# Four results of each block-product unit stored from GpSimd's queue instead of SyncE's

## The chip, the cores and the metric

The kernel runs on one core of one Trainium2 chip. The metric is device time in microseconds (us) of one execution. Three runs of the kernel before gave 3406.56, 3407.65 and 3411.39 us, so the median is 3407.65 us. A smaller number is better.

## The reference, cut to what matters

The input is `x` of 16 batches by 256 tokens by 512 channels, in fp32. Layer 0 is a decoder block: self attention, cross attention and an MLP. Layer 1 is an RWKV block: token mixing, a linear recurrence over the tokens, a gate and a channel mixing. The part that the change touches is the recurrence, with 32 heads of 16 channels:

```
def step(s, inp):
    k_l, v_l, w_l, r_l = inp
    a = k_l[..., :, None] * v_l[..., None, :]
    out = jnp.einsum('bhs,bhst->bht', r_l, faaaa * a + s)
    s_new = a + w_l[..., None] * s
    return (s_new, out)
```

The kernel does not step through 256 tokens. It cuts them into blocks of 8. Inside of a block it forms all products of r, k and the decays w directly; from block to block it carries the state with a scan. For each block the first part leaves four results:

- `rp`: r times the product of the decays from the block's start to the token;
- `ks`: k times the product of the decays from the token to the block's end;
- `tot`: the product of all eight decays of the block;
- `y`: what the block's own tokens add to the output.

## The kernel before, in words

Everything is recorded first as operations with a cost, an engine or a choice of engines, and the tiles read and written. A planner (`Sched.run`, L260) then places them one after the other: at each step it takes the operation that can start first by its own cost table, picks the engine where there is a choice, gives the tile a buffer, and emits the instruction. Each engine and each DMA queue runs its instructions strictly in that order. The planned costs therefore decide the order of all queues, and a changed cost in one place moves instructions far from it.

The phases are A (self attention), B (cross attention), C (MLP), D (token mixing: r, k, v, w, g to scratch in HBM) and E (the tail: state scan, gate, output projection, channel mixing). C and D are cut in two halves of eight batches: C0, D0, C1, D1. Between them runs a side stream of 16 units, recorded by `intra` (L1167): one unit covers four batches (`g`) and 128 channels (`q`). A partition holds one block of 8 tokens, so a tile is 128 blocks by 8 tokens by 128 channels in fp32, 512 KB. Units 1 to 8 (phase `I0`) run beside C1, units 9 to 16 (phase `I1`) beside the tail.

One unit loads K, R and W (L1188), multiplies K by the bonus `u` and by R (L1207, L1208), and doubles the reach of the decays in three rounds (L1212 to L1243). The products are recorded with `tt`, which is `sub` at L489: the planner puts them on VectorE (DVE) or on GpSimd (POOL), and in the trace all carry the line of `sub`, L492 for POOL. The reductions (L1209, L1213, L1222, L1239, L1254) are on DVE alone. After the third round the unit loads V (L1240), stores `rp`, `ks` and `tot` (L1244), forms the eight rows of Y (L1246 to L1256; the last one ends with a reduction on DVE, L1254) and stores `y` (L1257). `rp`, `ks` and `y` are 512 KB in rows of 512 bytes, `tot` is 64 KB.

All DMAs go through `dma` (L479). It records an operation on SP with a planned cost of 440 ns and emits `nc.sync.dma_start`; its line in the trace is L480. SP's queue holds 1218 DMAs, the loads of weights, of the units and of the tail among them, and the 64 stores of the units. When the DMA at its head waits for the engine that makes its data, those behind it wait too. The tiles K, R, W, V of the units have the tag `rk` with a quota of four (L1624), so the planner lets a next unit's load follow once a tile of the unit before was given up.

The tail reads back what the units stored, four units at a time since it works by batch with all channels: `states` loads `ks` (L1400) and `tot` (L1364), `reads` loads `rp` (L1450), `heads` loads `y` (L1479). Batches 12 to 15 need units 13 to 16.

Of the kernel before, what the change touches and what calls it, by code (L numbers as in the profile page):

```python
# [16 lines left out]
B, S, C = 16, 256, 512  # L17
# [168 lines left out]
class Sched:  # L186
# [73 lines left out]
    def run(self):  # L260
# [13 lines left out]
        def can(o):  # L274
            n = {}
            for h in o.tiles:
                if h.cls is not None and h.t is None:
                    k = h.phase, h.tag, h.cls
                    n[k] = n.get(k, 0) + 1
            for h in o.tiles:  # L280
                if h.cls is not None and h.t is None:
                    k = mem.why_not(h, n[h.phase, h.tag, h.cls])
                    if k is not None:
                        return k
            return None

        def put(o):
            k = can(o)
            if k is not None:
                waits.setdefault(k, []).append(o)  # L290
                return
            banks, t0 = 0, o.hold
            for h in o.tiles:
                if h.cls is not None and h.t is None:
                    t0 = max(t0, mem.ready(h))
                    banks += h.cls == "p"
            if banks > 1:
                t0 = max(t0, sorted(mem.banks.values())[banks - 1])
            o.t0 = {}
            for e, _, _ in o.alts:  # L300
                o.t0[e] = t0
                for d in o.deps:
                    p = ops[d]
                    o.t0[e] = max(o.t0[e], p.end + (self.SAME[e] if p.eng == e and not p.xfer else p.lat + self.LATE.get(e, 0.0)))
            for a in o.alts:
                ready[a[0]].append((o, a))
# [5 lines left out]
        while done < len(ops):  # L312
            best = None
            for e in engs:
                f, c = free[e], None
                for o, a in ready[e]:
                    s = o.t0[e] if o.t0[e] > f else f
                    if e in o.port and port > s:
                        s = port
                    if o.xfer and queues - self.AHEAD > s:  # L320
                        s = queues - self.AHEAD
                    for h in o.banks:
                        for e2, t in used.get(h, {}).items():
                            if e2 != e and t > s:
                                s = t
                    if len(o.alts) > 1:
                        s += o.bias.get(e, 0.0)
                    kx = (max(s - o.urge, f), o.prio, a[1])
                    if c is None or kx < c[0]:
                        c = (kx, o, a)  # L330
                if c is not None and (best is None or c[0] < best[0]):
                    best = c
            assert best is not None, "the streams block each other: " + str({k: [o.i for o in v][:3] for k, v in waits.items() if v})
            _, o, alt = best
            for a in o.alts:
                ready[a[0]].remove((o, a))
            k = can(o)
            if k is not None:
                waits.setdefault(k, []).append(o)
                continue  # L340
            o.eng, o.cost, fn = alt
            o.lat = self.LAT[o.eng]
            t0 = max(o.hold, o.t0[o.eng])
            woken = {}
            for h in sorted((h for h in o.tiles if h.cls is not None and h.t is None), key=lambda h: h.seq):
                if h.cls is not None and h.t is None:
                    t0 = max(t0, mem.ready(h))
                    mem.put(h)
                    woken[h.phase, h.tag, h.cls] = 1
            s = max(t0, free[o.eng])  # L350
            for h in o.banks:
                s = max([s] + [t for e2, t in used.get(h, {}).items() if e2 != o.eng])
            if o.eng in o.port:
                s = max(s, port)
                port = s + o.cost
            if o.xfer:
                s = max(s, queues - self.AHEAD)
            o.start, o.end = s, s + o.cost
            free[o.eng] = o.end
            for h in o.banks:  # L360
                used.setdefault(h, {})[o.eng] = o.end + o.lat
            if o.xfer:
                o.end = queues = max(o.end + self.START, queues) + o.xfer
            if not self.dry:
                fn()
                self.pin()
            for h in o.tiles:
                h.left -= 1
                if h.left == 0 and h.cls is not None:
                    mem.drop(h, o.end + o.lat)  # L370
                    woken[h.phase, h.tag, h.cls] = 1
                    woken[mem.SIZE[h.cls][0]] = 1
            done += 1
            for d in o.outs:
                p = ops[d]
                p.ndep -= 1
                if p.ndep == 0:
                    put(p)
            for k in woken:
                for p in waits.pop(k, []):  # L380
                    put(p)
# [21 lines left out]
def c_dma(nbytes, short=False):  # L403

    return nbytes / (146.0 if short else 290.0)


class Kern:
# [67 lines left out]
    def cols(self, ap, n, name):  # L476
        return self.konst([128, n], ap.rearrange("(k p) -> p k", p=128), name)

    def dma(self, h, out, in_, nbytes, r=(), w=None, short=False):  # L479
        o = self.emit("SP", 440.0, lambda: self.nc.sync.dma_start(out=out(), in_=in_()), r=r, w=[h] if w is None else w)  # L480
        o.xfer = c_dma(nbytes, short)
        return o

# [683 lines left out]
def intra(self, g, q, hin, hout, after, early=None):  # L1167
# [6 lines left out]
    def view(ap, t=8):  # L1174
        return bass.AP(tensor=ap.tensor, offset=ap.offset + g * 4 * S * C + q * 128, ap=[[8 * C, 128], [C, t], [1, 128]])
# [6 lines left out]

    def store(n, t, f, nb):
        h, ap = hout[n]
        self.dma(None, lambda: view(ap) if n != "tot" else bass.AP(tensor=ap.tensor, offset=ap.offset + g * 128 * C + q * 128, ap=[[C, 128], [1, 128]]), f, nb, [t], [(h, (g, q))])

    A = tile("A", [128, 8, 8, 8], "A")
    K, R, W = load("k"), load("r"), load("w")  # L1188
# [30 lines left out]
    for h in range(2):  # L1219
        o = 4 * h  # L1220
# [14 lines left out]
    for h in range(2):  # L1235
        o = 2 * h
# [5 lines left out]
    tt(512, lambda: K[:, 0:4], lambda: K[:, 0:4], lambda: W[:, 4:5].to_broadcast([128, 4, 128]), [K, W], [K])  # L1242
    tt(128, lambda: W[:, 0], lambda: W[:, 0], lambda: W[:, 4], [W], [W])  # L1243
    store("rp", R, lambda: R(), 524288), store("ks", K, lambda: K(), 524288), store("tot", W, lambda: W[:, 0], 65536)  # L1244
    yield
    Y = tile("Y", [128, 8, 128], "Y")  # L1246
    for t in range(8):
        n = t + 1
# [6 lines left out]
        if t in (3, 5):  # L1255
            yield  # L1256
    store("y", Y, lambda: Y(), 524288)  # L1257


# [481 lines left out]
```

## Time and profile before

| what | value |
|---|---|
| median of three runs | 3407.65 us |
| time of the profiled execution | 3407.0 us |
| its span, first to last instruction | 3405.2 us |
| granted TensorE clock, mean | 0.975 |
| PE busy | 3196.5 us, 94% |
| DVE busy | 2842.5 us, 83% |
| ACT busy | 1878.1 us, 55% |
| POOL busy | 1501.6 us, 44% |
| stores of the units, all on SP | 16 each of `s_rp`, `s_ks`, `s_y`, `s_tot` |
| first and last `s_rp` store | 2088.0 and 3136.3 us |

The span is what the trace covers; the execution's own time is 1.8 us longer. An engine's busy share is an average over stages with different limits: POOL's 44% is made of stretches with almost nothing and of stretches at 94%. What a change costs or gains is therefore read from the stretch in which it lies, and from what the next engine waits for there. A row like `POOL slot L492 <- DMA slot<-s_w` names the waiting engine, what its instruction writes and its line, and behind the arrow what it waited for: here a load from the scratch tensor `s_w`. `SPq` is SP's DMA queue.

### The profile page before, as it was taken

The page shows a single profiled execution, that of the slowest core. Times are in us where ns is not written, and L with a number is a line of the kernel's source. Part 1 is how long each engine was busy: PE and PEld are TensorE (multiplying, and loading weights), DVE is VectorE, ACT ScalarE, POOL GpSimd, SP SyncE. Part 2 cuts the span into 40 slices and gives each one's busy share as a digit, 9 for nine tenths or more (in the row PEclk, how much of TensorE's full clock was granted, in tenths as well). Part 3 has the DMA queues.
Part 4 walks back from the last instruction along what each step waited for, and adds up shares of the span by engine and source line. Part 5 has one row for each costly group of instructions (what it writes and reads, how often), then busy time and mean ns, then how long its engine had stood idle before and what let it go on. Part 6 is the DMA issues. An engine that isn't in the chain of part 4 may idle for free. (4 is left out here: it accounts for less than half of the span.)

```text
span 3405.2 us, 73366 instructions
## 1 busy us (share of the span) xinstructions
PE 3196.5 (94%) x27210; PEld 2627.1 (77%) x27210; DVE 2842.5 (83%) x6701; ACT 1878.1 (55%) x4750; POOL 1501.6 (44%) x1932
## 2 busy tenths in 40 slices
PE   7999999999999999899999999999799859999899
PEld 5788777777777777799998888999698745555577
DVE  7888888888888888876788889899889868888786
ACT  6666666666666666633334554434454547565654
POOL 3444444443444444300021127898112766767442
PEclk9999999999999999899999999999899969999999
DMA  3000000121111111310023554434345876765530
GB/s 101 26 26 32 27 29 28 35 79 44 45 45 45 45 45 54 104 33 13 32 75 125 170 180 131 124 117 121 106 152 160 251 230 189 211 195 177 172 120 32
DMA packets 321775, 334.21 MB, mean 98 GB/s; under 512 B 40294, under 2 KB 225166, under 8 KB 321418
## 3 DMA queue, kind: packets, MB, share of 16 engines
q1 hardware_dynamic: 321418, 329.52, 31.1%
q8 instruction: 216, 3.54, 0.4%
q14 instruction: 141, 1.16, 0.1%
HBM read 198.32 MB, written 131.10 MB: 97 GB/s over the span
## 5 line engine op out<-in xcount | busy, mean ns | idle before, releaser
L743 POOL TENSOR_SCALAR slot<-slot,k_rin 128x256 f32<-128x256 f32 x1024 | 489.2, 496 | 619.1 <-DVE k_rin L740 582.7
L492 POOL TENSOR_TENSOR slot<-slot,slot 128x512 f32<-128x512 f32 (+10 forms) x428 | 570.6, 1352 | 339.5 <-ACT slot L571 96.3
L737 ACT ACTIVATE slot<-slot,k_nmx 128x256 f32<-128x256 f32 x1024 | 507.8, 500 | 171.0 <-DVE k_nmx L736 148.5
L506 PE MATMUL bank<-slot,block 128*128 128x256 f32 x2048 | 584.8, 286 | 1.8 <-ACT slot L487 1.3
L507 PE MATMUL bank<-slot,block 128*128 128x256 f32 x2048 | 581.9, 284 | 2.1 <-DVE slot L578 1.4
L508 PE MATMUL bank<-slot,block 128*128 128x256 f32 x2048 | 580.9, 284 | 0.0
L506 PE MATMUL bank<-block,slot 128*128 128x512 f32 x1240 | 502.4, 405 | 4.4 <-DVE slot L577 2.9
L487 ACT ACTIVATE slot<-bank 128x512 f32<-128x512 f32 (+2 forms) x634 | 343.1, 571 | 291.0 <-PE bank L508 148.8
L508 PE MATMUL bank<-block,slot 128*128 128x512 f32 x1240 | 486.6, 392 | 4.5 <-DVE slot L578 2.7
L507 PE MATMUL bank<-block,slot 128*128 128x512 f32 x1240 | 486.4, 392 | 0.0
L506 PEld LDWEIGHTS bank<-slot,block 128*128 128x128 f32 x2048 | 393.5, 192 | 10.6 <-ACT slot L487 3.0
L507 PEld LDWEIGHTS bank<-slot,block 128*128 128x128 f32 x2048 | 393.6, 192 | 9.8 <-DVE slot L623 1.8
L736 DVE CUSTOM_DVE_ANT_0 slot<-slot,slot 128x256 f32<-128x256 f32 x1006 | 398.6, 443 | 0.0
L508 PEld LDWEIGHTS bank<-slot,block 128*128 128x128 f32 x2048 | 393.5, 192 | 0.0
L730 DVE SCALAR_TENSOR_TENSOR slot<-bank,slot 128x512 f32<-128x512 f32 x512 | 330.0, 680 | 53.4 <-PE bank L768 25.1
L756 PE MATMUL bank<-k_c,slot 128*128 128x128 f32 x2048 | 286.3, 280 | 17.6 <-POOL slot L743 13.4
L756 PEld LDWEIGHTS bank<-k_c,slot 128*128 128x128 f32 x2048 | 229.8, 142 | 88.5 <-POOL slot L743 57.5
L506 PE MATMUL bank<-slot,slot 128*128 128x256 f32 (+1 forms) x848 | 276.8, 326 | 13.9 <-ACT slot L577 11.5
L506 PEld LDWEIGHTS bank<-block,slot 128*128 128x128 f32 x1240 | 234.6, 189 | 65.4 <-issue 19.8
L507 PE MATMUL bank<-slot,slot 128*128 128x256 f32 (+1 forms) x848 | 275.5, 325 | 6.6 <-DVE slot L578 6.3
L508 PEld LDWEIGHTS bank<-block,slot 128*128 128x128 f32 x1240 | 233.8, 189 | 59.1 <-DVE slot L578 5.1
L508 PE MATMUL bank<-slot,slot 128*128 128x256 f32 (+1 forms) x848 | 275.0, 324 | 2.4 <-DVE slot L578 2.4
(203 smaller groups left out, 6467.7 us busy)
## 6 DMA issues: line engine op xcount, KB each, us to landing
slot<-in SPq DMA_DIRECT2D x153, 256.0 KB
slot<-x SPq DMA_DIRECT2D x64, 512.0 KB
x<-slot SPq DMA_DIRECT2D x48, 512.0 KB
slot<-in SPq DMA_DIRECT2D x32, 512.0 KB
sdr<-slot SPq DMA_DIRECT2D x128, 128.0 KB
slot<-sdr SPq DMA_DIRECT2D x32, 512.0 KB
s_k<-slot SPq DMA_DIRECT2D x16, 512.0 KB
s_w<-slot SPq DMA_DIRECT2D x16, 512.0 KB
```

The lines of the kernel that those rows point to most:

```text
L487: self.emit(("ACT", "DVE"), (c_act(n), c_dve(n)), (lambda: nc.scalar.activation(out=out(), in_=in_(), func=AF.Copy), lambda: nc.vector.ten ...
L492: self.emit(("DVE", "POOL"), (c_dve(n), c_pool(n)), (lambda: nc.vector.tensor_tensor(out=out(), in0=in0(), in1=in1(), op=op), lambda: nc.g ...
L506: nc.tensor.matmul(o, lhsT=lh, rhs=rh, start=first and i == 0, stop=False)
L507: nc.tensor.matmul(o, lhsT=lh, rhs=rl, start=False, stop=False)
L508: nc.tensor.matmul(o, lhsT=ll, rhs=rh, start=False, stop=last and i == k - 1)
L730: emit("DVE", c_dve(512), lambda j=j, T=T: nc.vector.scalar_tensor_tensor(out=T(), in0=ps[j](), scalar=-scale, in1=mask(), op0=ALU.mult, o ...
L736: emit("DVE", c_dve(256) + 80, lambda T=T, j=j, qt=qt: nc.vector.tensor_tensor_reduce(out=T[:, qt, :], in0=T[:, qt, :], in1=negb[:, qt, :] ...
L737: emit("ACT", c_act(256, 1, 1), lambda T=T, Et=Et, j=j, qt=qt: nc.scalar.activation(out=Et[:, qt, :], in_=T[:, qt, :], func=AF.Exp, scale= ...
L743: emit("POOL", 470, lambda jj=jj, qt=qt: nc.gpsimd.tensor_scalar(out=E[jj][:, qt, :], in0=E[jj][:, qt, :], scalar1=rin[:, qt, jj : jj + 1] ...
L756: nc.tensor.transpose(pt[:, k, 128 * qt : 128 * qt + 128], E[j][:, qt, 128 * k : 128 * k + 128], self.ident())
```

## The change

`dma` gets a flag `own`. With it the DMA is recorded on POOL with a planned cost of 1100 ns, and emitted with `nc.gpsimd.dma_start`. The unit's `store` sets the flag for `y`, `rp`, `ks` and `tot`, which is for all four. The planner's allowance behind a transfer (`LAT`) is kept at SP's 950 ns for any DMA, where POOL's own table entry is 65 ns. No data, size or address changes.

```
-            o.lat = self.LAT[o.eng]
+            o.lat = self.LAT["SP" if o.xfer else o.eng]
...
-    def dma(self, h, out, in_, nbytes, r=(), w=None, short=False):
-        o = self.emit("SP", 440.0, lambda: self.nc.sync.dma_start(out=out(), in_=in_()), r=r, w=[h] if w is None else w)
+    def dma(self, h, out, in_, nbytes, r=(), w=None, short=False, own=False):
+
+        e, c, q = ("POOL", 1100.0, self.nc.gpsimd) if own else ("SP", 440.0, self.nc.sync)
+        o = self.emit(e, c, lambda: q.dma_start(out=out(), in_=in_()), r=r, w=[h] if w is None else w)
         o.xfer = c_dma(nbytes, short)
         return o
...
     def store(n, t, f, nb):
         h, ap = hout[n]
-        self.dma(None, lambda: view(ap) if n != "tot" else bass.AP(...), f, nb, [t], [(h, (g, q))])
+        own = n in ['y', 'rp', 'ks', 'tot']
+        self.dma(None, lambda: view(ap) if n != "tot" else bass.AP(...), f, nb, [t], [(h, (g, q))], own=own)
```

The changed file is three lines longer below these places. In the two built programs the instructions stand as follows. SP's queue goes from 1218 to 1154 DMAs. POOL goes from 1932 to 1984 instructions: 64 DMAs more and 12 compute instructions fewer. DVE goes from 6701 to 6716, ACT from 3725 to 3722, PE stays at 21546. The streams are the same up to the end of the first unit; from there on they are in another order on every engine, PE included (of 16090 rows of PE's stream, equal neighbours merged, the first that differs is 11202).

More of the change, by code (lines that the diff above doesn't have):

```diff
@@ L1184, in store @@
         h, ap = hout[n]
-        self.dma(None, lambda: view(ap) if n != "tot" else bass.AP(tensor=ap.tensor, offset=ap.offset + g * 128 * C + q * 128, ap=[[C, 128], [1, 128]]), f, nb, [t], [(h, (g, q))])
+        own = n in ['y', 'rp', 'ks', 'tot']
+        self.dma(None, lambda: view(ap) if n != "tot" else bass.AP(tensor=ap.tensor, offset=ap.offset + g * 128 * C + q * 128, ap=[[C, 128], [1, 128]]), f, nb, [t], [(h, (g, q))], own=own)
     A = tile("A", [128, 8, 8, 8], "A")
```

## The prediction

> **What bounds the kernel now.** I read first the profile's slices, then the engines by stretch, then SP's waits, then one unit on POOL and SP in order of time, and last the chain.
>
> ```profile
> PE   7999999999999999899999999999799859999899
> POOL 3444444443444444300021127898112766767442
> DMA  3000000121111111310023554434345876765530
> ```
>
> A slice is 85 us. The units lie in slices 25 to 28 (2088 to 2400 us, beside the MLP) and 32 to 37 (the tail). PE is full in the first stretch; the tail is where it has holes.
>
> ```profile
> core 0: us, PE busy (x) PEld busy (x) DVE busy (x) ACT busy (x) POOL busy (x), PEclk, DMA share, GB/s
> 2200.00:2300.00 100.00, 99.81 (x640) 90.73 (x639) 92.47 (x133) 39.41 (x72) 93.94 (x72) 1.00 0.41 123
> 2300.00:2400.00 100.00, 99.62 (x646) 90.81 (x645) 95.17 (x141) 44.18 (x81) 79.07 (x64) 1.00 0.36 109
> 2400.00:2500.00 100.00, 79.28 (x452) 68.85 (x451) 82.03 (x152) 48.59 (x92) 16.23 (x20) 0.88 0.41 130
> 2700.00:2800.00 100.00, 56.60 (x1204) 46.35 (x1202) 70.54 (x121) 50.90 (x119) 64.83 (x60) 0.69 0.78 234
> 3000.00:3100.00 100.00, 91.63 (x1372) 61.27 (x1371) 86.95 (x160) 70.67 (x155) 69.74 (x64) 0.95 0.62 191
> ```
>
> So the first eight units run on a POOL that has little room (79 to 94%), under a PE that never stops; the second eight run on a POOL that is some 70% busy, under a PE that is 57 to 92% busy. Next, what SP's queue waited for, in each stretch, and what that made late:
>
> ```profile
> SPq L480 <- POOL slot L492: 150.8, 27, 21.6
> SPq L480 <- DVE slot L1254: 60.9, 15, 8.7
> ...
> SPq L480 <- POOL slot L492: 57.7, 14, 10.7
> SPq L480 <- DVE slot L1254: 14.4, 3, 8.4
> ...
>   POOL slot L492: 27.6, 6
> ...
> PE bank L1419 <- DMA block<-s_v: 29.2, 6, 14.2
> ```
>
> The first two lines are 2088 to 2650 us, the next two the tail: stores at the head of SP's queue that wait for POOL's product or DVE's last reduction of Y. Behind them stand the next unit's loads; the fifth line, of those who waited for the tensor s_w, says that POOL waited 27.6 us in all for a load of W. The last line is PE in the tail, waiting for loads that the units have no part in. Then the last unit, in order of time along the chain:
>
> ```profile
> 3133.78 2.51 POOL slot L492 x2
> 3136.31 3.51 DMA s_rp<-slot
> 3139.87 3.67 DMA slot<-s_rp
> ...
> 3146.29 6.76 POOL slot L492 x5
> 3153.05 3.53 DMA s_ks<-slot
> 3156.59 5.20 DMA slot<-s_ks
> 3161.82 0.88 DVE slot L1346 x2
> 3163.09 1.11 PE bank L1371 x4
> ```
>
> POOL finishes a product, the store lands, the tail loads it back, and only then PE goes on. From 3120 to 3163 us PE was busy 32.81 of 43 us. The last unit is thus on the path: if it comes later, the end comes later by nearly as much.
>
> **The price of a store on POOL.** No row of before has a DMA on POOL. From below the nearest is the same transfer issued by SP: 0.56 us for a store of rp, ks or y (medians 563, 558 and 555 ns). From above it is POOL's own pass over as many elements as a store moves, the product with `u` over 128x1024 fp32: 2.41 us in the first stretch. A store issues 1024 rows of 512 bytes, but computes on no element. Between ends a factor of four apart I take the geometric middle, 1.2 us, for all four stores; the tot store is a sixteenth of the rows, but its SP issue had a median of 1.24 us. Four stores: 4.8 us per unit, bounds 2.2 and 9.6.
>
> The Trainium skill, "DMA: Bandwidth & Descriptors", section "Latency and other measured facts", puts the first byte at about 1 us for a DMA from GpSimd and about 0.6 us from SP. By it alone, the two landings of the last unit would be 0.8 us later together. Against the change speaks "SBUF — State Buffer", section "SBUF: two separate sides", in its box on the trap that DVE blocks DMA: a two-port VectorE instruction keeps GpSimd from writing descriptors, and a DMA of about 620 ns took about 3100 ns beside one. The trace has DVE at 92 to 95% in the first stretch, but no run here shows such a block. By that rule the 64 stores would cost 64 x 2.5 = 160 us more of POOL.
>
> **The waits that move to POOL.** POOL runs in order. On SP the y stores waited 75.3 us in 18 waits for L1254, 4.7 us per unit. In the changed order most y stores stand behind some products of the next unit, so most of it passes under work; I keep a third, 1.5 us per unit (bounds 0 and 4.7). Behind the waiting store stand the next unit's products and the tail's other POOL work (L1346, L596), for which ACT, DVE and at last PE wait.
>
> **What the loads gain.** Freed of stores, K, R, W and V can issue sooner. POOL waited 27.6 us for W, 10.6 us for K and 1.6 us for R: 39.8 us in 16 units, 2.5 per unit. Their place still follows the planner's quota of four tiles, so I take half, 1.2 us per unit (bounds 0 and 2.5).
>
> **First stretch.** Net 4.8 + 1.5 - 1.2 = 5.1 us per unit, eight units 41 us. The `s_rp` stores were issued from 2088.0 to 2366.55 us, a period of 39.8 us, of which POOL was idle 14% (42.4 us of 2100 to 2400), 5.6 us per unit. Part of that idle is the very wait for W, part is waiting for DVE; I let half of the 41 be swallowed. The eighth unit then ends 20 us later. PE does not need it there: the covering work is the MLP's matmuls (99.6% busy) and it ends at 2400. What it meets is the change of phase at 2400 to 2500, where PE already lost 20.7 us, and whose buffers and POOL work come after the units in the queues. A third of the slip reaches PE: 7 us (bounds 0 and the whole 41).
>
> **Tail.** Again 41 us for units 9 to 16. The `s_rp` issues from 2901.3 to 3136.3 us are 58.8 us apart, and POOL is some 70% busy, so 17 us per unit are idle. If all idle could be used the slip is 0; if each idle piece is a wait inside the unit's own chain it is 41. I take half, 20 us, and it goes to the end one for one, by the chain above.
>
> **The last unit's stores.** Its ks now stands before the products of Y on POOL, and rp and tot behind them. Before it was the other way round: rp at 3136.31, ks at 3153.05. So the last thing that the tail waits for stands at the same place, plus a tot store ahead of it (1.2 us) and 0.6 us more issue: 2 us.
>
> **SP's own relief.** SP loses 48 x 0.56 + 16 x 1.24 = 47 us of issue. It counts only where PE waits for an SP load, 2700 to 2800 us, with 0.78 of the DMA engines' time taken. Five stores were issued there, 3.3 us: -3 us. The data to move stays, so I expect no more.
>
> The rule of the Trainium skill, "DMA: Bandwidth & Descriptors", section "Issuing engines are not separate DMA queues", says that another issuing engine saves only the sequencer's time. By it alone the sum would be -3 us.
>
> **The new order.** From the first unit's end on every engine's stream is resorted: 12 products move off POOL, DVE gets 15 instructions more. The same matmuls remain. What a resorting can give or take lies in the PE holes of the tail, 98 us from 2700 to 3300; I set it at 0, plus or minus 15.
>
> Sum: 7 + 20 + 2 - 3 = 26 us on the profiled execution's 3407.0 us: 3433. That execution is 0.65 us under the median of the runs, so 3434 us.
>
> **The rivals.**
> *Faster: the loads come early.* One mechanism: SP, without waiting stores, runs ahead, and the units lose all 39.8 us of load waits while PE loses most of its 29.2 us. For it: 150.8 us of SP waits on POOL alone. Against: in 2700 to 2800 the DMA engines are the limit, and POOL gets 4.8 us per unit of new work. It decides when POOL's price per store is below 0.6 us. Then 8 x (2.4 - 2.5) is nothing for the tail, and PE gains half of 29.2, with resorting some 20: 3387 us.
> *No change: all is swallowed.* POOL's 17 us of idle per unit take the 5.1 us, and the phase change hides the rest: 3407 plus or minus 7.
> *Much slower: a store costs POOL 2.4 us or more.* Then 9.6 + 1.5 - 1.2 = 9.9 us per unit, 79 us per half. With POOL at 94% in the first stretch nothing more is swallowed there; tail 60, first stretch 25, last unit 5: 3497 us. More is possible if DVE holds POOL off.
> That the stores do not move is excluded by the built program: 64 DMAs stand in POOL's stream.
>
> **How the numbers follow.** Chances: forecast 0.67, much slower 0.17, no change 0.06, faster 0.10. The forecast alone spans 3415 to 3465: bounds of the swallowed half in the tail (0 and 41) and of the resorting. Leaving out a tenth at each end, the range is 3404 to 3490. Within 0.2% (6.8 us) is what a measurement of this kernel can hardly tell from no change. Slower 0.84, same 0.06, faster 0.10.
>
> **What would show it.** Right: 48 DMAs on POOL at about 1.2 us each; the first stretch's unit period near 42 to 43 us instead of 39.8; the last unit's stores at 3165 to 3180 instead of 3136 to 3155; the time from the last store to the end unchanged at some 250 us. SP's waits on POOL L492 and DVE L1254 gone, waits of POOL on DVE L1254 in their place. Wrong: a price under 0.6 us, POOL waits for W, K and R at zero and a last unit no later than 3155 (faster or same), or POOL above 95% from 2100 to 2400 with units 45 us or more apart (much slower).

## The result and the profile after

Four runs of the changed kernel gave 3440.88, 3450.06, 3451.16 and 3451.22 us, a median of 3450.61 us. Four runs of the kernel before (the three above and one of 3410.71 us) gave a median of 3409.18 us. The ratio is 1.0111, with a 95% interval of 1.0096 to 1.0126: the change costs some 38 us by the ratio, 41 us by the medians. The profiled execution took 3451.16 us, its span is 3449.4 us, the mean granted clock 0.970 (0.975 before).

The slices of the changed kernel, in tenths of busy time. A slice is 86 us.

```profile
PE   7999999999999999899999999999699769988889
...
POOL 3444444444444444200021128898213766768442
...
DMA  3001001021111111300024563333444876655530
```

The last twelve digits of PE are 699769988889, before 799859999899: seven of them are below 9 where four were. The tail is where to look. The engines by stretch, in the changed kernel:

```profile
core 0: us, PE busy (x) PEld busy (x) DVE busy (x) ACT busy (x) POOL busy (x), PEclk, DMA share, GB/s
2200.00:2300.00 100.00, 98.52 (x620) 88.11 (x620) 90.31 (x129) 33.09 (x59) 90.54 (x71) 1.00 0.38 112
2300.00:2400.00 100.00, 98.17 (x643) 89.33 (x642) 91.19 (x138) 41.88 (x76) 89.56 (x76) 1.00 0.37 113
2400.00:2500.00 100.00, 72.68 (x392) 61.56 (x391) 84.86 (x147) 45.85 (x86) 33.88 (x32) 0.85 0.41 127
2700.00:2800.00 100.00, 63.85 (x1178) 54.23 (x1181) 74.06 (x121) 59.56 (x135) 62.39 (x56) 0.72 0.81 249
3000.00:3100.00 100.00, 84.59 (x1245) 55.33 (x1246) 81.94 (x146) 58.73 (x140) 65.70 (x60) 0.91 0.63 188
...
3100.00:3200.00 100.00, 75.74 (x958) 47.24 (x957) 73.83 (x119) 48.40 (x103) 75.21 (x66) 0.89 0.54 165
```

The table of before has no row for the last stretch. It is this one:

```profile
3100.00:3200.00 100.00, 89.72 (x788) 53.51 (x787) 82.78 (x159) 55.81 (x127) 56.86 (x56) 0.93 0.59 182
```

Read the PE column against the table of before. Beside the MLP PE loses some 1.3 us per 100 from 2200 us on (98.52 for 99.81, 98.17 for 99.62); from 2100 to 2200 us, which the tables leave out, it loses 6.2 (93.80 for 99.99). At the change of phase it loses 6.6 us (72.68 for 79.28), from 3000 to 3100 us 7.0, and from 3100 to 3200 us 14.0, the most of all. From 2700 to 2800 us it gains 7.3. Over the whole span PE was busy 3208.7 us for the same 27210 instructions, before 3196.5. So 32 of the 44 us by which the span grew are idle time of PE; no run tells what made its busy time 12 us longer.

What SP's queue waited for, first from 2088 to 2650 us, then (the last two lines) in the tail from 2650 to 3300 us:

```profile
SPq L482 <- DVE slot L893: 107.7, 7, 22.4
SPq L482 <- DVE slot L1257: 83.8, 8, 28.3
...
SPq L482 <- POOL slot L494: 1.8, 8, 0.2
...
SPq L482 <- PE bank L1422: 77.5, 13, 14.7
...
SPq L482 <- POOL slot L494: 3.9, 7, 1.3
```

The waits on POOL's product (L494, which was L492) went from 150.8 and 57.7 us to 1.8 and 3.9. SP did not become free by that. In all it waited 484.4 us in the first stretch and 325.8 in the tail, before 467.5 and 307.5: its wait for L1257 (L1254 before) grew from 60.9 to 83.8 us although no `y` store is left in the queue, and in the tail its wait for L1422 (L1419 before) grew from 31.5 to 77.5 us. At the head stands now a load that waits for a buffer.

POOL's own waits: the stores of `y` from 2088 to 2650 us, and, from the view of the tensor `s_w`, what is left of the wait for W:

```profile
POOL s_y L482 <- DVE slot L1257: 12.1, 2, 11.4
...
  POOL slot L494: 1.7, 1
```

The wait for W went from 27.6 to 1.7 us. In its place POOL waited 17.6 us in 4 waits for DVE's last reduction of Y, over the whole run. PE in the tail:

```profile
PE bank L1461 <- DVE slot L1359: 12.9, 2, 11.2
PE bank L1422 <- ACT slot L1349: 10.1, 2, 9.8
PE bank L1422 <- ACT slot L1430: 9.7, 1, 9.7
...
PE bank L1422 <- DMA block<-s_v: 5.2, 3, 2.5
```

The wait for `s_v` went from 29.2 to 5.2 us, as an earlier load would do it. But three waits of about 10 us each, on results of DVE and ACT, stand in its place; before, the longest wait of PE on DVE or ACT in this stretch was 7.4 us.

The price of a store on POOL, from the views of the four scratch tensors (minimum, median, maximum in ns):

```profile
L482 POOL DMA_DIRECT2D s_rp<-slot x16: 841/881/982, 2106.6 to 3190.8; - x16
...
L482 POOL DMA_DIRECT2D s_ks<-slot x16: 816/888/922, 2105.4 to 3179.9; - x16
...
L482 POOL DMA_DIRECT2D s_y<-slot x16: 834/862/1030, 2104.4 to 3192.6; - x16
...
L482 POOL DMA_DIRECT2D s_tot<-slot x16: 579/597/762, 2107.4 to 3190.2; - x16
```

All 64 cost 16 x (0.881 + 0.888 + 0.862 + 0.597) = 52 us of POOL. The last stores went out at 3179.9 to 3192.6 us; before, they went out at 3136.3 to 3155.3. POOL's stream around them, in order of time:

```profile
3164.48 0.69 POOL L1349 TENSOR_SCALAR slot<-slot,k_em 128x512 f32<-128x512 f32 x1 [8.19 <-DMA slot<-sdr]
...
3171.48 7.62 POOL L494 TENSOR_TENSOR slot<-slot,slot 128x1024 f32<-128x1024 f32 x5
3179.20 0.72 POOL L598 TENSOR_TENSOR k_lnrs<-k_lnrs,k_mhalf 128x2 f32<-128x2 f32 x1
3179.88 0.90 POOL L482 DMA_DIRECT2D s_ks<-slot  x1
...
3182.97 7.30 POOL L494 TENSOR_TENSOR slot<-slot,slot 128x512 f32<-128x512 f32 x5
3190.21 0.59 POOL L482 DMA_DIRECT2D s_tot<-slot  x1
3190.80 0.90 POOL L482 DMA_DIRECT2D s_rp<-slot  x1
3192.59 0.84 POOL L482 DMA_DIRECT2D s_y<-slot  x1 [0.90 <-DVE slot L1257]
```

The stores themselves take 3.2 of these 29 us. Above the last unit's products stands an operation of the tail, L1349, that waited 8.19 us for a load of the tail.

A slip is best followed by one kind of event that every version has in the same number. The table gives how much later than in the kernel before (the first row) certain stores of SP start in the profiled executions. The first column is the last but one store of `x`, at the end of the MLP, the others are five of the 16 stores of the output (first, fourth, eighth, ninth, last).

| kernel | MLP's end | out 1 | out 4 | out 8 | out 9 | out last |
|---|---|---|---|---|---|---|
| before, us | 2390.9 | 2857.3 | 2984.2 | 3150.0 | 3201.2 | 3401.4 |
| changed | +9.9 | +16.5 | +10.4 | +20.1 | +38.3 | +43.9 |
| new order, stores on SP (e2) | +2.0 | +7.8 | +5.3 | +7.7 | +26.7 | +30.2 |
| old order, stores on POOL (e1) | +6.3 | +8.2 | +12.2 | +12.3 | +12.5 | +15.4 |
| old order, POOL price doubled (e8) | +22.5 | +27.6 | +32.0 | +31.5 | +32.4 | +34.1 |
| old order, price without stores (e9) | +1.3 | +0.6 | +1.7 | -1.1 | -0.5 | +0.1 |
| old order, rp alone on POOL (e13) | +6.0 | +10.1 | +14.4 | +14.3 | +14.8 | +14.2 |
| rp alone, with its own plan (e5) | -1.9 | -14.4 | -17.7 | -10.4 | -9.0 | -6.2 |

The rows below the second belong to the experiments. Differences of a few us need care: one execution differs from another before the first unit is done. By the same instruction of PE, at 2100 us the changed kernel was 1.1 us ahead of the kernel before, e2 4.4, e1 7.0, e8 5.5, e9 6.4 and e13 3.0. What counts is how much a row grows.

### The profile page after: what moved, and what is told of

Its sections match the earlier page's. It is cut to its first block, busy times and chain, and to the rows that moved or that the text cites. A ratio compares the mean times of both kernels' runs of the same rounds, so it can differ in the third digit from the quotient of the medians.

```text
span 3449.4 us, 73352 instructions
## 1 busy us (share of the span) xinstructions
PE 3208.7 (93%) x27210; PEld 2633.2 (76%) x27210; DVE 2862.0 (83%) x6716; ACT 1874.3 (54%) x4747; POOL 1545.9 (45%) x1984
## 3 DMA queue, kind: packets, MB, share of 16 engines
q0 software_dynamic: 7424, 26.22, 2.4%
## 5 line engine op out<-in xcount | busy, mean ns | idle before, releaser
L494 POOL TENSOR_TENSOR slot<-slot,slot 128x512 f32<-128x512 f32 (+11 forms) x435 | 578.4, 1349 | 333.7 <-ACT slot L573 110.6
L758 PE MATMUL bank<-k_c,slot 128*128 128x128 f32 x2048 | 286.1, 280 | 17.6 <-POOL slot L745 12.8
L758 PEld LDWEIGHTS bank<-k_c,slot 128*128 128x128 f32 x2048 | 229.9, 142 | 88.5 <-POOL slot L745 57.7
```

Of the source, the lines that this page charges most:

```text
L494: self.emit(("DVE", "POOL"), (c_dve(n), c_pool(n)), (lambda: nc.vector.tensor_tensor(out=out(), in0=in0(), in1=in1(), op=op), lambda: nc.g ...
L758: nc.tensor.transpose(pt[:, k, 128 * qt : 128 * qt + 128], E[j][:, qt, 128 * k : 128 * k + 128], self.ident())
```

## The experiments

In all of them the same products, sums and transfers are computed, and nothing is left out. Each diff is against the changed kernel unless it says otherwise. What the planner books for a DMA (engine and cost) and which queue emits it are two different things in `dma`, so each can be changed alone. "Old order" means that the booking is that of the kernel before, so every engine has its instructions in the old order.

**e1: the stores on POOL, in the old order.**

```
-        e, c, q = ("POOL", 1100.0, self.nc.gpsimd) if own else ("SP", 440.0, self.nc.sync)
+        e, c, q = ("SP", 440.0, self.nc.gpsimd) if own else ("SP", 440.0, self.nc.sync)
```

> The stores are issued by POOL, but recorded for the planner as before (SP, 440 ns), so that all other instructions keep the order of the kernel before, and each store stands on POOL where it stood in time. Theory of the forecast (the price and the waits on POOL's queue make the loss): at least 25 of the 41 us, 3430 to 3450 us. Rival, resorting (the new plan makes the loss): at most 12 us over before, 3405 to 3421 us, with the stores on POOL at the same 0.87 us each.

Measured: 3424.70 us against 3406.51, ratio 1.0046 [1.0030, 1.0062], or 16 us. That lies between the two ranges expected. A store cost POOL 873 ns (rp), 871 (ks), 872 (y) and 601 (tot), as in the changed kernel. The row of its stretch 2200 to 2300 us, and what the `y` stores waited for:

```profile
2200.00:2300.00 100.00, 97.28 (x609) 87.24 (x608) 87.26 (x123) 36.26 (x68) 96.39 (x77) 0.98 0.38 116
```

```profile
L482 POOL DMA_DIRECT2D s_y<-slot x16: 839/872/923, 2097.9 to 3167.9; - x16
...
  DVE slot L1257: 14.1, 7
```

POOL is at 96.39 us of 100 (93.94 before). By the table the slip is +6.3 at the MLP's end, some 12 at the fourth output store, and from there to the end only 3 more.

**e2: the new order, the stores on SP.** The booking of the change, but nothing is issued by POOL.

```
-        e, c, q = ("POOL", 1100.0, self.nc.gpsimd) if own else ("SP", 440.0, self.nc.sync)
+        e, c, q = ("POOL", 1100.0, self.nc.sync) if own else ("SP", 440.0, self.nc.sync)
```

> The opposite half: the planner books the stores on POOL at 1100 ns, as in the changed kernel, so the order of every engine is the changed kernel's, but SP issues them. Theory of the forecast: most of the loss goes, 3405 to 3420 us. Rival, resorting: it stays, 3430 to 3450 us, with no DMA on POOL at all.

Measured: 3438.90 us against 3406.51, ratio 1.0086 [1.0068, 1.0104], or 29 us. So most of the loss comes without a single DMA on POOL. e1 and e2 together make 45 us, with an interval of about 37 to 53 (the two half-widths of 6 us added as squares); the change itself makes 38 [33, 43]. Within these intervals the two parts account for the whole. One reserve: in e2 the stores stand in SP's queue, at the places that the new plan gives them, and SP waited 60.0 us for POOL's product from 2088 to 2650 us and 23.3 in the tail (before 150.8 and 57.7). No run has the new order without that.

Where e2 loses it is seen in the table: 19.0 of its 30.2 us between the eighth and the ninth output store. The changed kernel loses 18.2 there, e1 0.2. The stretch in e2, and then POOL's stream in it:

```profile
3100.00:3200.00 100.00, 71.90 (x829) 44.21 (x828) 75.21 (x127) 50.49 (x119) 60.48 (x52) 0.85 0.56 173
```

```profile
3152.37 0.69 POOL L1349 TENSOR_SCALAR slot<-slot,k_em 128x512 f32<-128x512 f32 x1 [8.26 <-DMA slot<-sdr]
...
3159.10 7.63 POOL L494 TENSOR_TENSOR slot<-slot,slot 128x1024 f32<-128x1024 f32 x5
3166.83 0.70 POOL L598 TENSOR_TENSOR k_lnrs<-k_lnrs,k_mhalf 128x2 f32<-128x2 f32 x1
...
3169.70 7.30 POOL L494 TENSOR_TENSOR slot<-slot,slot 128x512 f32<-128x512 f32 x5
```

PE is busy 71.90 us of this 100, before 89.72. One of its waits from 3100 to 3260 us, which the kernel before does not have there, is for the `ks` that the tail reads back:

```profile
PE bank L1422 <- DMA slot<-s_ks: 9.5, 1, 9.5
```

The stream is that of the changed kernel, with the same wait of some 8 us ahead of the last unit's products. The last `s_rp` store goes out at 3180.2 us, 44 us later than before, and between the `s_rp` stores of units 13 and 14 lie 88.8 us (2990.46 to 3079.29), before 65.8 (2957.98 to 3023.74). POOL was no busier than before in that time (98.40 us of 2950 to 3100, before 103.23). Over the tail it waited longer for loads of `sdr` ahead of L1349: 41.3 us in 11 waits, in the changed kernel 44.7 in 11, before 19.5 in 8. So the new plan lets the last units come later, and their readers in the tail wait. That it is these waits of POOL that make them late is argued; no run moves L1349 alone.

**e3 and e4: only one half of the units.** Units 1 to 8 (`g < 2`) or 9 to 16 (`g >= 2`) as in the change, the others as before.

```
-        own = n in ['y', 'rp', 'ks', 'tot']
+        own = g < 2
```

> Only the 32 stores of units 1 to 8 go through POOL; units 9 to 16 store through SP as before. The shifts in the two traces say that 20 us are lost by the middle of D1 and 24 more in the tail. If the first half's loss is carried to the end, 3425 to 3432 us; if the tail takes it up in its holes, 3405 to 3415 us; if the plan of the tail is a lottery of its own, anything from 3400 to 3440.

> Only the 32 stores of units 9 to 16 go through POOL. Up to 2600 us it is the kernel before. Forecast: tail 20 + 2 us, 3425 to 3435 us. Resorting: the new tail's plan decides, about 3415 to 3440 us; a price of 32 x 0.8 us of POOL alone could give no more than 26 us.

Measured: e3 3425.13 us, ratio 1.0041 [1.0025, 1.0057], 14 us; e4 3422.89 us, 1.0034 [1.0017, 1.0052], 12 us; both against 3406.51. Together they make 26 us of the 38, with an interval of about 18 to 34. e3 lies at the lower edge of its first range, e4 just under the forecast's. Both halves cost about the same, each with the order that its own booking gave, so neither run separates the queue from the order.

**e9 and e8: the price of the stores, without them and on top of them.** In the old order two small operations on POOL, on a scratch tile of their own, are added behind each of the four stores. In e9 the stores stay on SP, in e8 they are on POOL as in e1. The lines of e8 against e1:

```
+        def issue():
+            q.dma_start(out=out(), in_=in_())
+            if own:
+                self.nc.gpsimd.tensor_tensor(out=self.idle[:, 0:1], in0=self.idle[:, 2:3], in1=self.mhalf[:, 0:1], op=ALU.pow)
+                self.nc.gpsimd.tensor_copy(out=self.idle[:, 1:2], in_=self.mhalf[:, 0:1])
```

> The order of the kernel before, the stores on SP as before; behind each store POOL runs two small instructions on scratch of its own (a power of 128x1, a copy of 128x1), about 0.7 + 0.2 us by the rows of the norm's power and of the 128x2 copy, as long as the 0.87 us that a store took on POOL. They wait for nothing. Theory P (the 16 us of the first experiment are the time that POOL's stream is held): 10 to 18 us over before. Theory L (they are the longer way to landing, 4.5 to 5.2 us instead of 3.5, and the waits on the stores' semaphores): at most 6 us.

> As the first experiment (order of before, stores issued by POOL), with the same two small instructions behind each store, so that POOL pays about double. Theory P: another 12 to 20 us over the first experiment, 28 to 36 over before. Theory L: 16 to 22 over before. If POOL had room to swallow it (the half that the forecast took): 24 over before.

Measured: e9 3409.89 us against 3407.28, ratio 1.0009 [0.9996, 1.0023], so 8 us at most; the two operations took 549 and 186 ns (medians), 47 us in all. In its trace PE goes from 6.4 us ahead at 2100 us to 0.8 behind at 2400, and stays there. Theory P had asked for 10 to 18 us and fell. e8 3443.06 us, ratio 1.0106 [1.0089, 1.0123], 36 us, which is 20 more than e1 for 598 + 204 ns, 51 us in all. Here theory L fell (16 to 22 us) and P had its range. Neither theory fits both runs: the same added time costs more where the stores already stand in the stream. The rows of 2100 to 2400 us, of before, of e9 and of e8:

```profile
2100.00:2400.00 300.00, 299.42 (x1930) 272.57 (x1930) 276.12 (x399) 122.92 (x223) 257.64 (x198) 1.00 0.39 117
```

```profile
2100.00:2400.00 300.00, 295.43 (x1882) 266.98 (x1882) 272.65 (x392) 119.38 (x217) 269.23 (x255) 0.99 0.39 116
```

```profile
2100.00:2400.00 300.00, 284.40 (x1769) 255.50 (x1767) 261.83 (x367) 109.62 (x198) 286.04 (x278) 0.97 0.37 113
```

In this stretch POOL goes from 257.64 us (before) to 269.23 (e9), 271.87 (e1) and 286.04 (e8); PE goes from 299.42 to 295.43, 291.05 and 284.40. The first 12 us more of POOL cost PE 4 (e9), the next 17 cost it 11 (e9 to e8). With stores in the stream the same POOL time costs PE 4 us more than without (e1 against e9). How it reaches PE is named by PE's waits from 2100 to 2400 us. The row of before, and that of e8:

```profile
PE bank L613 <- ACT slot L601: 0.6, 2, 0.4
```

```profile
PE bank L623 <- ACT slot L611: 10.7, 9, 3.1
```

This is the layer norm ahead of the MLP. POOL computes its reciprocal root (L596 before) between two steps of DVE, ACT applies it (L601; L611 here), and PE transposes the result (L613; L623). In e1 the same wait was 4.3 us, in e9 3.9. That the root stands behind the units' stores in POOL's stream is the smaller part of it: over the seven norms from 2088 to 2420 us it started, all together, 3.5 us after DVE's step before it, in e9 and in e1 4.6, in e13 (below) 5.8 and in e8 8.0. What grew more is the step of DVE behind it (L597; L599 in the changed file), on 128x2 elements. Its rows before, in e13 and in the changed kernel:

```profile
L597 DVE SCALAR_TENSOR_TENSOR k_lnnb<-k_lnmv,k_lnrs x7: 151/247/954, 2134.3 to 2358.5; 128x2 f32<-128x2 f32 x7
```

```profile
L599 DVE SCALAR_TENSOR_TENSOR k_lnnb<-k_lnmv,k_lnrs x7: 151/1249/2574, 2131.3 to 2363.4; 128x2 f32<-128x2 f32 x7
```

```profile
L599 DVE SCALAR_TENSOR_TENSOR k_lnnb<-k_lnmv,k_lnrs x7: 138/1152/5432, 2148.5 to 2377.6; 128x2 f32<-128x2 f32 x7
```

The long ones end where a product of POOL ends. In e13 the longest, on DVE, and POOL's three products of that time:

```profile
2131.26 2.57 DVE L599 SCALAR_TENSOR_TENSOR k_lnnb<-k_lnmv,k_lnrs 128x2 f32<-128x2 f32 x1
```

```profile
2130.07 3.75 POOL L494 TENSOR_TENSOR slot<-slot,slot 128x512 f32<-128x512 f32 x3
```

Both end at 2133.8 us. The same holds over the whole of the traces of before, e1, e8, e9, e13 and the changed kernel: of the 80 such steps of each, those without an instruction of POOL beside them took 0.16 us at most, and each of the 10 to 14 that took over 0.3 us ended within 0.03 us of the end of an instruction of POOL. The seven steps took 2.6 us together before, 5.1 in e9, 6.6 in e1, 7.9 in e13 and 12.1 in e8, and PE's wait rises in the same order: 0.6, 3.9, 4.3, 5.9 and 10.7. A store, or any work added to POOL, thus moves POOL's products against these steps. How much of the loss that makes is argued; no run changes the step alone, and PE's idle time in the stretch is more than this wait.

In the tail the doubled price cost nothing beyond e1: e8's slip grows from 27.6 us at the first output store to 34.1 at the last, 6.5 us, in e1 by 7.2.

**e12 and e13: which of the stores.** In the old order, e12 has rp, ks and tot on POOL and y on SP; e13 has rp alone on POOL. The line of e13, against e1:

```
-        own = n in ['y', 'rp', 'ks', 'tot']
+        own = n == 'rp'
```

> Order of all engines as in the kernel before; rp, ks and tot are issued by POOL, the 16 y stores stay on SP. Theory 'waits in the stream' (the 16 us of e1_old_order_pool over before come mostly from the y stores, which wait in POOL's own stream for DVE's last reduction, in the trace of that run 14.1 us of idle time ahead of y stores): at most 8 us over before, 3409 to 3415. Rival 'each store costs' (the 16 us come from POOL's issue time, the same for every store): three quarters of 16 or a little more, 10 to 16 us over before, 3417 to 3423, and hardly any wait of POOL on DVE's last reduction left in the trace.

> Order as in the kernel before; only the 16 rp stores are issued by POOL. It is to tell where the 7 us gain of e5_rp_only came from. If from the queue (SP's loads no longer stand behind a store that waits for POOL's product): 5 to 8 us under before here too, 3399 to 3402, with POOL's waits for W below their 27.6 us of before. If from the plan that the other booking gave: no gain, 0 to 5 us over before, 3407 to 3412.

Measured: e12 3420.50 us against 3405.56, ratio 1.0043 [1.0029, 1.0056], 15 us; e13 3415.95 us, 1.0037 [1.0024, 1.0050], 13 us. e13 lies above both of its ranges. Without the `y` stores the loss of e1 is still there: the theory that it comes from the `y` stores' waits for DVE, 14.1 us in e1's row, fell. Sixteen `rp` stores alone, 14 us of POOL, cost 13 [8, 17] us, nearly as much as all 64. That the loss grows with the number of stores is not borne out either. In e13's trace POOL is no busier than before from 2100 to 2400 us (256.56 us), yet PE waits as in e1. ACT's row and PE's, 2088 to 2420 us:

```profile
ACT slot L603 <- DVE k_lnnb L599: 12.2, 6, 3.8
```

```profile
PE bank L615 <- ACT slot L603: 5.9, 7, 2.6
```

Before, the first was 3.8 us in 4 waits. Why the `rp` stores do this and the three others add so little wasn't settled. One thing that goes the other way with them is POOL's wait for the loads of W, K and R: 49.3 us in e13 (before 39.8), with `ks` and `tot` on POOL too 17.9 (e12), with all four 13.1 (e1). Whether that pays for the other stores was not tested.

**e5: rp alone, with the plan that its booking gives.** Booked on POOL and issued by POOL, the others as before.

```
-        own = n in ['y', 'rp', 'ks', 'tot']
+        own = n == 'rp'
```

> Only the 16 rp stores go through POOL (0.87 us each, 7 us of POOL a half). By price alone 4 us over before. The order is again a new one: by the theory of resorting anything from 10 under before to 25 over.

Measured: 3400.55 us against 3407.28, ratio 0.9980 [0.9971, 0.9990]: 7 us faster, the best of all versions and faster than both kernels. Its row of the change of phase:

```profile
2400.00:2500.00 100.00, 90.43 (x491) 76.86 (x490) 89.02 (x167) 49.74 (x95) 31.26 (x31) 0.93 0.46 148
```

PE is busy 90.43 us here, before 79.28; by the table it is 14.4 us ahead at the first output store. e13 has the same stores on the same queue in the old order and is 13 us slower than before, so the gain comes from the plan that the booking of sixteen stores led to, not from the queue.

**e6: another order for nothing.** The stores stay on SP, booked there at 450 instead of 440 ns.

```
-        e, c, q = ("POOL", 1100.0, self.nc.gpsimd) if own else ("SP", 440.0, self.nc.sync)
+        e, c, q = ("SP", 450.0, self.nc.sync) if own else ("SP", 440.0, self.nc.sync)
```

> The kernel before with one number changed: the planner books the 64 stores at 450 ns on SP instead of 440. Nothing moves to POOL, but the plan comes out in another order. If resorting as such costs (a tuned order is lost with any change), 10 to 30 us over before; if only this particular booking on POOL makes a bad order, within 8 us of before, on either side.

Measured: 3407.16 us against 3407.28, ratio 0.9999 [0.9989, 1.0008]. The order changes on every engine, and the time does not. This resorting costs nothing; that of the change does.

**e10: all four on POOL, booked otherwise.** 870 ns instead of 1100, which is what a store took in the changed kernel, and DVE may work beside it in the plan.

```
-        e, c, q = ("POOL", 1100.0, self.nc.gpsimd) if own else ("SP", 440.0, self.nc.sync)
+        e, c, q = ("POOL", 870.0, self.nc.gpsimd) if own else ("SP", 440.0, self.nc.sync)
...
+        if own:
+            o.port = ()
```

> All four results are issued by POOL as in the change, but the planner books 870 ns instead of 1100 for each, which is what a store took on POOL in the changed kernel, and lets DVE work beside it. Theory 'the plan is a draw' (most of the loss comes with whichever order the planner makes, the issue itself costs 16 us): anywhere from 3410 to 3445, and another order than that of the changed kernel. Rival 'the POOL's load' (any order with 64 stores on POOL loses the same, since the streams must give up that time somewhere): 3440 to 3455, as the changed kernel.

Measured: 3429.74 us against 3405.56, ratio 1.0067 [1.0051, 1.0083], 23 us. The same 64 stores on the same queue cost 16, 23 [17, 28] or 38 us, by the order alone. The first two intervals overlap; the third lies above both.

**e7: rp and ks on ACT's queue.**

```
-        e, c, q = ("POOL", 1100.0, self.nc.gpsimd) if own else ("SP", 440.0, self.nc.sync)
+        e, c, q = ("ACT", 440.0, self.nc.scalar) if own else ("SP", 440.0, self.nc.sync)
...
-        own = n in ['y', 'rp', 'ks', 'tot']
+        own = n in ['rp', 'ks']
```

> rp and ks are issued from ACT's queue, booked at 440 ns on ACT; y and tot stay on SP. ACT is 33 to 42% busy from 2100 to 2400 us in the changed kernel, where POOL is 86 to 91%. Theory (a waiting store costs by what stands behind it on its engine): ACT's work behind a store that waits for POOL's product is in part what DVE and PE wait for, so 0 to 15 us over before, 3407 to 3422. Rival (an engine with room costs nothing, and SP's loads come earlier): 5 to 15 us under before, 3392 to 3402, faster than both kernels.

Measured: 3409.77 us against 3405.56, ratio 1.0014 [0.9999, 1.0029]. The 5 to 15 us of gain are excluded; whether it costs up to 10 us or nothing is not. An engine with room did not make the loads' head start count.

## Why the prediction was right or wrong

The forecast was 3434 us, range 3404 to 3490, slower at 0.84. Measured were 3450.61: slower, inside the range, 17 us above the forecast. The likeliest case held, and the terms of its sum were these.

*The price of a store* was put at 1.2 us, between 0.56 and 2.41. It is 0.86 to 0.89 us for 512 KB and 0.60 us for tot, 3.2 us per unit instead of 4.8. The row of SP's issue was the nearer end. (The prediction calls tot a sixteenth of the rows; 64 KB of 512 are an eighth. Its price did not use that.) The rule of "SBUF — State Buffer", section "SBUF: two separate sides", that a two-port instruction of DVE holds up the writing of descriptors, is not seen here: the longest of the 64 stores took POOL 1.03 us, with DVE at 90% in the first stretch. How much of that DVE time was two-port work was not counted. The prediction had priced it at 160 us and had left it out.

*The waits that move to POOL*, 1.5 us per unit: 17.6 us in 16 units are 1.1. Right in size, but e12 shows that they are not what costs.

*What the loads gain*, 1.2 us per unit: the wait for W fell by 25.9 us, 1.6 per unit. K is still waited for, 10.6 us as before. SP's wait of 83.8 us on L1257 says why SP gained no more: its loads wait for the buffers.

*First stretch.* The period of the units was to grow from 39.8 to between 42 and 43 us: from 2106.6 to 2406.4 us there are seven periods of 42.8. A third of the slip was to reach PE, 7 us. From 1.1 us ahead at 2100 us the changed kernel goes to 9.9 behind at the MLP's end, 11 us; e1 goes from 7.0 ahead to 6.3 behind, 13 us. So the term was under-sized by some 5 us, and its place was wrong. The prediction let PE run untouched beside the MLP and pay at the change of phase. e1 pays beside the MLP (PE 291.05 us of 300, before 299.42) and next to nothing at the change of phase (78.72 us of 100, before 79.28); the changed kernel, with its new order, pays at both. The prediction did name L596 as behind a waiting store, but not that DVE's step after it can last until a product of POOL ends.

*Tail*, 20 us one for one from POOL's load. This is over-sized. In the old order the slip grows by 7.2 us from the first to the last output store (e1), and by 6.5 when the price is doubled (e8): the added time of POOL beyond that was taken up by its idle time in the tail, as far as these two runs show. The prediction's bounds were 0 and 41.

*The last unit's stores and the time behind them.* They were to come at 3165 to 3180 us and came at 3180 to 3193. From the last store to the span's end it is 250 us before and 257 after, as said; the last unit is on the path.

*SP's relief*, -3 us. PE's wait for `s_v` fell by 24 us, so the loads do come earlier, but other waits took the place. The rule of "DMA: Bandwidth & Descriptors", section "Issuing engines are not separate DMA queues", that only the sequencer's time is saved, was put at the same 3 us; e1 shows that the issuing engine's own stream costs more than that.

*The new order* is the step that failed. It said: "I set it at 0, plus or minus 15." e2 measured 29 us [23, 35] with the order changed and no store on POOL, twice the bound, and e1 and e2 together put two thirds of the loss down to the order. The rest of the sum, 7 + 20 + 2 - 3 = 26, stood for POOL's load, which e1 measured at 16 [10, 21]. So the total came near by luck, through two errors of opposite sign: POOL's load too dear by 10 us, its tail above all, the order too cheap by 29. The size of an order's effect was not to be had from before's profile: e6 and e5 resort as well and give 0 and -7. But the prediction gave it a bound from PE's holes in the tail alone, all holes being 98 us, and took a sixth of them without a row to say why; and it did not ask where in the new order the last unit stands, though it had named the last unit as the path.

*The rivals.* "The loads come early" had the head start right (the waits for W and `s_v` fell) and the price above its point of 0.6 us; it is excluded. "All is swallowed" nearly holds for POOL's bare time (e9, 3 us, at most 8), not for the stores. "A store costs POOL 2.4 us or more" is excluded by the rows of the stores.

## What to carry to other kernels

Where a planner orders all queues by booked costs, booking a transfer on another engine is two changes, and the order can be the larger one; keep the order and change the queue, then the reverse, before either is given the credit or the blame. Then look at where the last producer on the path stands in the new order, here a unit whose results came some 40 us later, rather than at the waits that the stores were known to cause, which fell. And a store on a computing engine's queue is not paid by its 0.9 us alone: 16 of them cost nearly as much as 64. Look at the small steps that the bottleneck waits for, here a layer norm's step on DVE, and at what runs beside them.

## What the runs showed of the hardware

A store of 512 KB in rows of 512 bytes took POOL 0.86 to 0.89 us of its stream and landed after 4.6 to 5.7 us (medians of `y`, `rp` and `ks`); from SP, the last unit's two stores landed 3.51 and 3.53 us after issue. The difference, 1.1 to 2.2 us a landing, is more than the 0.8 us that the prediction worked out for two. On ACT's queue the issue of `rp` took 0.52 us (median, e7).

A step of DVE on 128x2 elements took 0.14 to 0.15 us at the shortest and up to 5.43 us in the changed kernel, from 2158.76 to 2164.19 us, while POOL ran one product after another; the last one that it outlasted ended at 2164.16.

What the queues moved, in the changed kernel:

```profile
q1 hardware_dynamic: 269194, 303.30, 28.6%
q0 software_dynamic: 7424, 26.22, 2.4%
```

Before, q1 held 321418 packets and 329.52 MB. The 26.2 MB of the units' results went as 52224 packets there and as 7424 on POOL's queue, some 3.5 KB each instead of 502 bytes. I had not expected that; no run shows that it changed the time.
